# A graph layer with residual and layer norm on one Trainium2 core: broadcasts of packed slots cut into eight, 14 gather buffers, PSUM banks dealt three and two, and late-planned SP transfers

## The chip, the cores and the metric

The kernel runs on one core of a Trainium2 chip. The time is device microseconds for one launch. Before the change the median of three runs is 502.47 us (501.62 to 507.94). One further run was profiled; all views of a profile below come from it.

## The reference, cut to what matters

```python
N, E, D = 6250, 100000, 128          # nodes, edges, features; edges are sorted by dst
def layer(X, src, dst, edge_types, W_data, b_data, W_control, b_control, W_self, b_self):
    Xs = X[src]
    m_data = Xs @ W_data.T + b_data
    m_ctrl = Xs @ W_control.T + b_control
    msg = jnp.where((edge_types == 0)[:, None], m_data, m_ctrl)
    agg = jax.ops.segment_sum(msg, dst, num_segments=X.shape[0])
    return jax.nn.relu(agg + (X @ W_self.T + b_self))
x = _layernorm(x + layer(x, ...), axis=-1)
```

## The kernel before, in words

**Table.** Every node's two messages (data and control) are computed once: 49 blocks of 128 nodes, two blocks at a time (25 steps `q`), as x times the two weights on TensorE (L483), with the result split into three bf16 parts that add up to the f32 value. The parts stay in SBUF as `m3` (98 tiles of 128 rows by 384 columns) and are also stored to DRAM as `table` (L499). A step's product lies in PSUM in a bank of ring `g` or ring `a`.

**Windows.** The first 27 x 160 nodes (`NW`, `WN`) are summed without touching DRAM for each edge. A window of 160 nodes has up to 21 x 128 edges. They are ordered into a grid of 98 source tiles by 32 slots (`R`) in `ranks`: one-hot tiles (`hots`, L681) are summed on TensorE (L692, bank `rk`), VectorE reduces the sums to slot numbers (L706), and matmuls (L742, bank `vt`) drop each edge's source and target into its slot. ScalarE copies the result out (`vs`), SP stores it to DRAM (`packed`, L762), and SP reads one window's 32 x 98 slots back, broadcast to all 128 partitions (`rows`, L893: 784 KB written, one contiguous run of 6272 bytes read 128 times). The windows go in eight groups, `GROUPS = [1, 2] + [4] * 6`: `ranks` and the store are made for a group, the broadcast for a window.

In `sums`, VectorE turns `rows` into a one-hot of source rows (L901) and `to_d` into a one-hot of targets (`hot2`, L909). Then 25 times per window: *stage 1*, up to four matmuls (L922) that pick 128 messages from `m3` into a PSUM bank of ring `g`; a copy to bf16 by ScalarE (L425, `gs`); *stage 2*, seven matmuls (L936, L939) that add them up by target into the window's bank of ring `a`. Edges that find no slot go in a short list: `sr` is gathered from `table` by GpSimd (L851), and SP copies its halves into `gl` (L858), which is the last of the 25 steps.

**Gathered blocks.** The remaining nodes are 16 blocks of 125. For these GpSimd gathers 128 messages at a time from `table` (`t_msg`, L1016, 263 times, 8 buffers) and TensorE adds them by target (L1023, one bank `ga`).

**Closing.** `close` reduces a window's or block's bank over its three parts (L551), adds x (`xr`, loaded at L524 and L531), norms, and stores (L602, L606). The x columns of the own-node product come in `xc`, `xb` and `t_xc` (L887, L534, L1000).

**Order.** Nothing runs in the order of the source. Every operation is handed to `Plan.add` with an engine, a planned duration, a due time and the buffers that it reads and writes. `Plan.run` is a list scheduler: an engine takes, of the operations whose buffers are ready at the earliest possible time, the one with the smallest due; it never waits for a due time. What comes out is one fixed order of instructions for each engine, and on the chip each engine runs its own order, waiting at each instruction for what it needs. So an instruction whose data are later on the chip than in the plan holds up everything behind it on its engine; for SP, which issues nearly all plain transfers, this is everything behind it in the queue. `T0 = 36`, `TW = 13` are the planned start of window 0 and the planned time of a window; `when` is the due time of a group's `ranks`.

PSUM's eight banks are `vt` 1, `rk` 1, `ga` 1, `a` 1 and `g` 4.

Of the kernel before, what the change touches and what calls it, by code (L numbers as in the profile page):

```python
# [21 lines left out]
P = 128  # L22
# [21 lines left out]
R = 32  # L44
# [38 lines left out]
class Op:  # L83
    __slots__ = ("alts", "due", "lat", "deps", "after", "left", "ready", "start", "end", "out",
                 "index", "engine")

    def __init__(self, alts, due, lat):
        self.alts, self.due, self.lat = alts, due, lat
        self.deps, self.after, self.out = [], [], []


class Plan:
    HOP = {"PE": 0.22, "ACT": 0.15, "DVE": 0.11, "POOL": 0.12, "SP": 0.12}
    OWN = {"DVE": 0.09, "ACT": 0.12}
    OTHER = 0.5

    def __init__(self):
        self.ops, self.rings = [], {}

    def add(self, engine, dur, fn, due, r=(), w=(), lat=0.0):  # L100
# [24 lines left out]
        return op  # L125
# [4 lines left out]
    def run(self):  # L130
# [31 lines left out]
        while len(order) < n:  # L162
# [79 lines left out]
def sums_over_windows(ctx, tc, x, xt, edges, w, bias, out, total):  # L242
# [16 lines left out]
    def C(shape, dtype, name):  # L259
        return Buf(plan, const, shape, dtype, name, 1)  # L260

    T0 = 36.0
    TW = 13.0
    LAT = 0.2
    G0, G1 = 0.0, -4
    GC = 1.3
    SPD = 0.45


# [7 lines left out]
    add("ACT", 0.1, lambda: A.dma_start(b1.t, bias), 0.0, [], [b1], lat=2.5)  # L277

# [83 lines left out]
    def count_rows():  # L362
# [8 lines left out]
    vec(0.5, 1, lambda: V.tensor_copy(row_i.t, row_f.t), [row_f], [row_i])  # L371
    er = C([NBD, RL, 3], I32, "er")
    add("POOL", 1.0, lambda: G.indirect_dma_start(
        out=er.t.rearrange("p k c -> p (k c)"), out_offset=None,
        in_=edges.rearrange("(p k) c -> p (k c)", k=RL),
        in_offset=bass.IndirectOffsetOnAxis(ap=row_i.t[:, 0:1], axis=0)),
        0.5, [row_i], [er], lat=3.5)
# [3 lines left out]
    vec(0.6, RL, lambda: V.tensor_copy(dst_f.t, er.t[:, :, 1]), [er], [dst_f])  # L381
    vec(0.6, RL, lambda: V.tensor_scalar(less.t, dst_f.t, bound_p.t, None, op0=ALU.is_lt,
# [15 lines left out]
    def load_edges(b, n, out_, due, buf, key, engine):  # L398
# [13 lines left out]

    left = C([1, D3], F32, "left")
# [3 lines left out]
    add("ACT", 0.4, lambda: A.copy(brows.t[:1], b1.t), 0.5, [b1], [brows])  # L417
    vec(0.5, D3, lambda: V.tensor_sub(left.t, b1.t, brows.t[:1]), [b1, brows], [left])
    add("ACT", 0.4, lambda: A.copy(mid.t, left.t), 0.5, [left], [mid])
    vec(0.5, D3, lambda: V.tensor_sub(brows.t[2 * R : 2 * R + 1], left.t, mid.t), [left, mid],  # L420
        [(brows, 2)])
# [19 lines left out]
    XB = [12, 12, 12, 13]  # L441
    XC = 4 * WN
    xts = []
# [167 lines left out]
    def ranks(gi, w0, nw, when, step, engines):  # L611
# [237 lines left out]
        for pr in range(nh):  # L849
            sr = B(work, [P, D3], BF16, "sr", 2)  # L850
            add("POOL", GC, lambda pr=pr, sr=sr: G.indirect_dma_start(  # L851
                out=sr.t[: room(pr)], out_offset=None, in_=table[:, :],
                in_offset=bass.IndirectOffsetOnAxis(ap=at.t[: room(pr), pr : pr + 1], axis=0)),
                d3 + 1, [(at, pr), table_b], [sr], lat=2.0)
            for i in range(2 * pr, min(2 * pr + 2, nw)):
                q = 64 * (i % 2)
                gl = B(work, [P, D3], BF16, "gl", 8)
                add("SP", SPD, lambda gl=gl, sr=sr, q=q: S.dma_start(gl.t[64:], sr.t[q : q + 64]),  # L858
                    d3 + 2 + pr, [sr], [(gl, "s")], lat=2.0)
                gls.append(gl)  # L860
# [23 lines left out]
    def sums(gi, w0, nw, placed):  # L884
# [5 lines left out]
        for i in range(nw):  # L890
            due = T0 + (w0 + i) * TW
            sp = B(work, [P, R, NT], BF16, "rows", 3, R * NT)
            add("SP", SPD, lambda i=i, sp=sp: S.dma_start(  # L893
                sp.t.rearrange("p r c -> p (r c)"),
                packed[gi, i // 2, (i % 2) * 64 : (i % 2) * 64 + R, :]
                .rearrange("r c -> (r c)")[None, :].to_broadcast([P, R * NT])),
                due - 12, [(packed_b, gi)], [sp], lat=3.0)
            half = R // 2
# [7 lines left out]
            for ci, (c0, c1) in enumerate(zip(cuts, cuts[1:])):  # L906
# [51 lines left out]
    def gathered(bis, when, step):  # L958
# [37 lines left out]
        for j, bi in enumerate(bis):  # L996
# [6 lines left out]
            for k in range(nt):  # L1003
                at = start + step * k
                kk = j * nt + k
                if k % KB == 0:
# [209 lines left out]
```

## Time and profile before

| what | value |
|---|---|
| median of 3 runs | 502.47 us |
| profiled execution: its own time | 505.74 us |
| its span, first to last instruction | 504.2 us |
| mean granted TensorE clock | 0.959 of full |
| TensorE matmul busy | 453.6 us (90%) |
| VectorE, ScalarE busy | 394.9 us (78%), 349.0 us (69%) |
| GpSimd busy | 299.2 us (59%) |
| bytes moved by DMA | 76.83 MB, mean 152 GB/s |
| broadcasts `rows<-packed` | 27 issues, SP, 784 KB each |
| gathers `t_msg<-table` | 263 issues, GpSimd, mean 1057 ns |

TensorE's row counts a matmul from its issue to its modelled end, so a busy TensorE may still have gaps between matmuls; the number of matmuls in a stretch says more. The chain of waits is followed back from the last instruction: at each step to what released it.

### The profile page before, as it was taken

Reading aid. Unit: us, or ns where it says so; the run is one execution under the profiler, and the core shown is the slowest. Engines: PE = TensorE matmul, PEld = TensorE weight load, DVE = VectorE, ACT = ScalarE, POOL = GpSimd, SP = SyncE. Lnnn points to the kernel's source line nnn. Section 1 sums busy time; section 2 is a strip of 40 time slices with the busy share of each in tenths; the row PEclk is TensorE's granted clock in tenths of the full one; section 3 lists DMA queues with packets and bytes.
Section 4 is the critical chain, followed back from the end, with each engine's and each line's share of the span. In section 5 each row is a group of like instructions: output and inputs, shape, how many; then the busy total and the mean of one; then the engine's idle time right before and its main releaser. Section 6 shows DMA issues by size and latency. Waiting matters only on the chain.

```text
span 504.2 us, 26935 instructions
## 1 busy us (share of the span) xinstructions
PE 453.6 (90%) x11461; PEld 364.8 (72%) x11461; DVE 394.9 (78%) x1271; ACT 349.0 (69%) x891; POOL 299.2 (59%) x290
## 2 busy tenths in 40 slices
PE   4999986996999998999699999999899999897990
PEld 2666654884778787787598877878678887686880
DVE  6599987998898988989598899888948787553343
ACT  2476763763767876778486788777867778595881
POOL 1000057775467687857676677777676757776720
PEclk9999996998799999999899999999989999898997
DMA  4399977346552466634655256662654426644320
GB/s 145 122 287 342 292 149 241 100 106 208 143 149 66 132 172 179 179 87 134 195 160 171 64 139 195 200 169 69 195 154 130 153 68 155 225 116 135 79 69 19
DMA packets 63117, 76.83 MB, mean 152 GB/s; under 512 B 21000, under 2 KB 52893, under 8 KB 62989
## 3 DMA queue, kind: packets, MB, share of 16 engines
q1 hardware_dynamic: 49147, 47.35, 29.8%
q0 software_dynamic: 13456, 27.42, 21.3%
q8 instruction: 91, 1.49, 1.2%
q10 hardware_dynamic: 386, 0.26, 0.2%
q14 instruction: 37, 0.30, 0.2%
HBM read 60.50 MB, written 13.17 MB: 146 GB/s over the span
## 4 chain that ended last, share of the span: by engine, by line
PE 67%; DMA 16%; DVE 7%; ACT 5%; issue 2%; SPq 1%; POOL 0%; ACTq 0%; DVEq 0%; POOLq 0%
PE g L922 20%; PE a L936 17%; PE rk L692 8%; DMA rows<-packed 7%; PE ga L1023 7%; DMA t_msg<-table,t_idx 6%; PE g L483 3%; PE a L939 3%; PE vt L742 3%; ACT gs L425 3%; DMA packed<-vs 2%; DVE rows L901 1%; ACT to_d L432 1%; PE ga L692 1%; PE a L508 1%
## 5 line engine op out<-in xcount | busy, mean ns | idle before, releaser
L1016 POOL DMA_INDIRECT t_msg<-table,t_idx x263 | 278.0, 1057 | 113.8 <-PE ga L1023 42.5
L425 ACT CAST gs<-g 128x384 bf16<-128x384 f32 x639 | 270.2, 487 | 103.3 <-PE g L922 81.3
L922 PE MATMUL g<-m,rows 128*32 128x384 bf16 x2646 | 261.2, 338 | 7.2 <-DVE rows L901 5.3
L936 PE MATMUL a<-gs,hot 128*32 128x384 bf16 x2592 | 259.9, 335 | 2.8 <-ACT gs L425 1.9
L922 PEld LDWEIGHTS <-rows 128*32 128x32 bf16 x2646 | 159.5, 135 | 22.2 <-DVE rows L901 6.4
L939 PE MATMUL a<-gs,hot 128*32 128x128 bf16 x1944 | 164.1, 222 | 0.0
L1023 PE MATMUL ga<-t_msg,t_hot 128*32 128x384 bf16 x1036 | 125.7, 332 | 16.7 <-DMA t_msg<-table,t_idx 10.7
L936 PEld LDWEIGHTS <-hot 128*32 128x32 bf16 x2700 | 121.9, 97 | 24.8 <-issue 7.9
L706 DVE TENSOR_REDUCE slot<-rk 128x4 f32<-128x392 f32 (+1 forms) x138 | 76.8, 556 | 23.9 <-PE rk L692 12.5
L939 PEld LDWEIGHTS <-hot 128*32 128x32 bf16 x2025 | 86.8, 99 | 10.7 <-issue 0.7
L692 PE MATMUL rk<-hots,tri 128*32 128x392 bf16 (+1 forms) x588 | 73.1, 327 | 0.7 <-issue 0.7
L692 PE MATMUL rk<-hots,rest 128*32 128x392 bf16 (+1 forms) x556 | 68.6, 328 | 2.6 <-DVE slot L706 2.6
L1023 PEld LDWEIGHTS <-t_hot 128*32 128x32 bf16 x1036 | 53.2, 98 | 23.7 <-issue 19.5
L909 DVE TENSOR_TENSOR hot<-iota_b,to_d 128x1280 bf16<-128x1280 bf16 (+1 forms) x81 | 67.6, 842 | 0.1
L851 POOL DMA_INDIRECT sr<-table,at x14 | 16.7, 1191 | 46.8 <-DMA xr<-in_x 38.6
L901 DVE TENSOR_SCALAR rows<-rows,pid 128x1568 bf16<-128x1568 bf16 x54 | 34.3, 638 | 12.8 <-DMA rows<-packed 12.7
L1010 DVE TENSOR_TENSOR t_hot<-iota_b,t_code 128x768 bf16<-128x768 bf16 (+2 forms) x47 | 24.7, 526 | 19.3 <-PE g L922 11.2
L681 DVE TENSOR_TENSOR hots<-iota_b,st 128x784 bf16<-128x784 bf16 (+1 forms) x83 | 38.6, 487 | 0.5 <-PE vt L742 0.4
L692 PEld LDWEIGHTS <-rest 128*32 128x32 bf16 x624 | 28.1, 98 | 10.6 <-issue 8.3
L692 PEld LDWEIGHTS <-tri 128*32 128x32 bf16 x672 | 30.1, 99 | 3.7 <-issue 1.4
L551 DVE TENSOR_REDUCE s<-a 128x128 f32<-128x384 f32 x27 | 15.0, 557 | 21.2 <-ACT bs L425 7.7
L425 ACT CAST m<-g 128x512 bf16<-128x512 f32 x20 | 11.6, 587 | 13.8 <-PE g L491 13.8
(188 smaller groups left out, 545.4 us busy)
## 6 DMA issues: line engine op xcount, KB each, us to landing
rows<-packed SPq DMA_DIRECT2D x27, 784.0 KB
table<-m SPq DMA_DIRECT2D x12, 768.0 KB
t_msg<-table,t_idx POOLq DMA_INDIRECT x263
rows<-in_xt SPq DMA_DIRECT2D x8, 256.0 KB
xc<-in_xt SPq DMA_DIRECT2D x6, 320.0 KB
gl<-sr SPq DMA_DIRECT2D x27, 48.0 KB
xr<-in_x SPq DMA_DIRECT2D x5, 256.0 KB
out<-xr SPq DMA_DIRECT2D x5, 256.0 KB
```

The source lines that it names most:

```text
L425: [("ACT", act(cols), lambda: A.copy(o(), src())), ("DVE", dve(cols), lambda: V.tensor_copy(o(), src()))], None, None, due, r, w, lat)
L681: lambda k=k, kn=kn, ci=ci, hs4=hs4: V.tensor_tensor(hv(ci)[:, k - ks[ci] : k - ks[ci] + kn].rearrange("p k w (c d) -> p (k w) c d", d=2), ...
L692: T.matmul(acc.t[R * j : R * j + R, c * wide : c * wide + wide], wt.t[:, R * j : R * j + R], one(k).rearrange("p w c -> p (w c)"), start=s ...
L706: vec(due, len(m) * wide, lambda r=r, m=m: V.tensor_reduce(slot.t[:, r:KT:L, :], acc.t[:, : len(m) * wide].rearrange("p (k w c) -> p k w c ...
L901: add("DVE", dve(half * NT, 0.335), lambda sp=sp, rs=rs: V.tensor_scalar(sp.t[:, rs], sp.t[:, rs], pid1.t, None, op0=ALU.is_equal), due - ...
L909: lambda i=i, hot2=hot2, s4=s4, c0=c0, c1=c1: V.tensor_tensor(hot2.t[:, c0:c1].rearrange("p g (c d) -> p g c d", d=2), iota1_b.t.rearrange ...
L922: T.matmul(gp.t[R * t : R * t + R, :D3], sp.t[:, :, 4 * g + t], m3.t[:, 4 * g + t, :], start=True, stop=True)
L936: T.matmul(a.t[R * j : R * j + R, :D3], hot2.t[:, g, R * j : R * j + R], gs.t, start=g == 0, stop=False, skip_group_check=True)
L939: T.matmul(a.t[R * c : R * c + R, D3:], hot2.t[:, g, P:], gs.t[:, c * D : (c + 1) * D], start=False, stop=last, skip_group_check=True)
L1010: vec(at + 1, kn * P, lambda hot=hot, kk=kk, kn=kn, s4=s4: V.tensor_tensor(hot.t.rearrange("p k (c d) -> p k c d", d=2), iota1_b.t[:, :P]. ...
L1016: add("POOL", GC, lambda m=m, kk=kk: G.indirect_dma_start(out=m.t, out_offset=None, in_=table[:, :], in_offset=bass.IndirectOffsetOnAxis(a ...
L1023: T.matmul(ga.t[R * i : R * i + R, :D3], hot.t[:, k % KB, R * i : R * i + R], m.t, start=k == 0, stop=False, skip_group_check=True)
```

## The change

Six things are edited together.

1. The broadcast of a window's slots is issued as eight transfers (`RP`) of 16 partitions each, due 0.9 us apart from 14 us ahead of the window, in place of one due 12 us ahead. VectorE's L901 still needs all of them.
2. `t_msg` has 14 buffers in place of 8. To make room in SBUF, the biases `b1` and `left` now lie in the ring of `two`, and the edge rows `er` in the ring of `xc`.
3. Ring `a` has two PSUM banks in place of one, ring `g` three in place of four; the table's steps are dealt 10 to `a` and 15 to `g` (5 and 20 before).
4. The planner adds a `slack` to the time at which an SP operation with a due time over 60 counts as ready: 6 us for loads of edges and x and for stores, 3 us for `gl`, 2 us for the store of `packed`; and 3 us for the gather of `sr` on GpSimd. It moves the operation back in SP's or GpSimd's order; no instruction is added for it.
5. The planned extra latency of a ScalarE or VectorE copy out of PSUM (`LAT`) is 0.1 in place of 0.2.
6. `when` is 0 in place of 3 for group 0 and 8 in place of 18 for group 1.

```diff
+    SLACK = dict.fromkeys(("t_raw", "win", "xc", "t_xc", "xr", "xrg", "xb", "out"), 6.0)
+    SLACK.update(gl=3.0, packed_b=2.0)
+    FROM = 60.0
...
+        kind = [(i[0] if isinstance(i, tuple) else i).name for i in w] or ["out"]
+        if engine == "SP" and due > self.FROM:
+            op.slack = self.SLACK.get(kind[0], 0.0)
...
-                    o.ready = max(o.ready, op.end + lag)
+                    o.ready = max(o.ready, op.end + lag + o.slack)
...
-    LAT = 0.2
+    LAT = 0.1
+    RP, RA, RS = 8, 14, 0.9
...
-    b1 = C([1, D3], F32, "b1")
+    early = lambda: B(work, [P, 48 * R], BF16, "two", 2, 48 * R)
+    b1_, left_ = early(), early()
...
-    er = C([NBD, RL, 3], I32, "er")
+    er_ = B(work, [P, XC], F32, "xc", 2, XC)
...
-        mp = B(ps, [P, 512], F32, *(("a", 1) if q % 5 > 3 else ("g", 4)))
+        mp = B(ps, [P, 512], F32, *(("a", 2) if q % 5 > 2 else ("g", 3)))
...
-                d3 + 1, [(at, pr), table_b], [sr], lat=2.0)
+                d3 + 1, [(at, pr), table_b], [sr], lat=2.0).slack = 3.0
...
-            add("SP", SPD, lambda i=i, sp=sp: S.dma_start(
-                sp.t.rearrange("p r c -> p (r c)"),
-                packed[gi, i // 2, (i % 2) * 64 : (i % 2) * 64 + R, :]
-                .rearrange("r c -> (r c)")[None, :].to_broadcast([P, R * NT])),
-                due - 12, [(packed_b, gi)], [sp], lat=3.0)
+            for j in range(RP):
+                add("SP", SPD, lambda i=i, sp=sp, j=j: S.dma_start(
+                    sp.t[P // RP * j : P // RP * (j + 1)].rearrange("p r c -> p (r c)"),
+                    packed[gi, i // 2, (i % 2) * 64 : (i % 2) * 64 + R, :]
+                    .rearrange("r c -> (r c)")[None, :].to_broadcast([P // RP, R * NT])),
+                    due - RA + RS * j, [(packed_b, gi)], [(sp, ("p", j))], lat=2.0)
...
-            a = B(ps, [P, 512], F32, "a", 1)
+            a = B(ps, [P, 512], F32, "a", 2)
...
-                gp = B(ps, [P, 512], F32, "g", 4)
+                gp = B(ps, [P, 512], F32, "g", 3)
...
-                m = B(work, [P, D3], BF16, "t_msg", 8)
+                m = B(work, [P, D3], BF16, "t_msg", 14)
...
-            when, step, engines = 3.0, 0.9, ["SP"]
+            when, step, engines = 0.0, 0.9, ["SP"]
         elif gi == 1:
-            when, step, engines = 18.0, 1.1, ["SP", "ACT"]
+            when, step, engines = 8.0, 1.1, ["SP", "ACT"]
```

More of the change, by code (lines that the diff above doesn't have):

```diff
@@ L84 @@
     __slots__ = ("alts", "due", "lat", "deps", "after", "left", "ready", "start", "end", "out",
-                 "index", "engine")
+                 "index", "engine", "slack")
     def __init__(self, alts, due, lat):
-        self.alts, self.due, self.lat = alts, due, lat
+        self.alts, self.due, self.lat, self.slack = alts, due, lat, 0.0
         self.deps, self.after, self.out = [], [], []
@@ L260, in C @@
         return Buf(plan, const, shape, dtype, name, 1)
+    XC = 4 * WN
     T0 = 36.0
     TW = 13.0
-    LAT = 0.2
+    LAT = 0.1
     G0, G1 = 0.0, -4
@@ L274, in sums_over_windows @@
     w_sb = C([D, D3], F32, "w_sb")
-    b1 = C([1, D3], F32, "b1")
+    early = lambda: B(work, [P, 48 * R], BF16, "two", 2, 48 * R)
+    b1_, left_ = early(), early()
+    b1 = lambda: b1_.t.bitcast(F32)[:1, :D3]
+    left = lambda: left_.t.bitcast(F32)[:1, :D3]
     add("ACT", 0.1, lambda: A.dma_start(w_sb.t, w), 0.0, [], [w_sb], lat=2.5)
-    add("ACT", 0.1, lambda: A.dma_start(b1.t, bias), 0.0, [], [b1], lat=2.5)
+    add("ACT", 0.1, lambda: A.dma_start(b1(), bias), 0.0, [], [b1_], lat=2.5)
     iota_f = C([P, P], F32, "iota_f")
@@ L371, in sums_over_windows @@
     vec(0.5, 1, lambda: V.tensor_copy(row_i.t, row_f.t), [row_f], [row_i])
-    er = C([NBD, RL, 3], I32, "er")
+    er_ = B(work, [P, XC], F32, "xc", 2, XC)
+    er = lambda: er_.t.bitcast(I32)[:NBD, : RL * 3].rearrange("p (k c) -> p k c", c=3)
     add("POOL", 1.0, lambda: G.indirect_dma_start(
-        out=er.t.rearrange("p k c -> p (k c)"), out_offset=None,
+        out=er_.t.bitcast(I32)[:NBD, : RL * 3], out_offset=None,
         in_=edges.rearrange("(p k) c -> p (k c)", k=RL),
         in_offset=bass.IndirectOffsetOnAxis(ap=row_i.t[:, 0:1], axis=0)),
-        0.5, [row_i], [er], lat=3.5)
+        0.5, [row_i], [er_], lat=3.5)
     dst_f = C([NBD, RL], F32, "dst_f")
@@ L380, in sums_over_windows @@
     in_row = C([NBD, 1], F32, "in_row")
-    vec(0.6, RL, lambda: V.tensor_copy(dst_f.t, er.t[:, :, 1]), [er], [dst_f])
+    vec(0.6, RL, lambda: V.tensor_copy(dst_f.t, er()[:, :, 1]), [er_], [dst_f])
     vec(0.6, RL, lambda: V.tensor_scalar(less.t, dst_f.t, bound_p.t, None, op0=ALU.is_lt,
@@ L410, in load_edges @@
         add(engine, dur, fn, due, [first] if b else [], [(buf, key)], lat=2.0)
-    left = C([1, D3], F32, "left")
     mid = C([1, D3], BF16, "mid")
@@ L416, in sums_over_windows @@
     vec(0.2, D3, lambda: V.memset(brows.t, 0.0), [], [brows], 0.3)
[L417 to L420, printed above, removed]
+    add("ACT", 0.4, lambda: A.copy(brows.t[:1], b1()), 0.5, [b1_], [brows])
+    vec(0.5, D3, lambda: V.tensor_sub(left(), b1(), brows.t[:1]), [b1_, brows], [left_])
+    add("ACT", 0.4, lambda: A.copy(mid.t, left()), 0.5, [left_], [mid])
+    vec(0.5, D3, lambda: V.tensor_sub(brows.t[2 * R : 2 * R + 1], left(), mid.t), [left_, mid],
         [(brows, 2)])
@@ L441, in sums_over_windows @@
     XB = [12, 12, 12, 13]
-    XC = 4 * WN
     xts = []
```

## The prediction

> **What bounds the kernel now.** I read the head of the page first, then busy time in equal stretches of 20 us, the waits of TensorE, the chain of waits in order of time, and the waits of SP's queue.
>
> ```profile
> span 504.2 us, 26935 instructions
> PE 453.6 (90%) x11461; PEld 364.8 (72%) x11461; DVE 394.9 (78%) x1271; ACT 349.0 (69%) x891; POOL 299.2 (59%) x290
> PEclk9999996998799999999899999999989999898997
> ```
>
> TensorE is busy for 90% of the span and no other engine comes near, so time can only come out of TensorE's gaps and of the slices where its granted clock falls below 9 tenths. The stretches say where these lie; the first column after the times is TensorE busy, with its matmuls in brackets, and the clock stands behind POOL.
>
> ```profile
> 60.00:80.00 20.00, 14.98 (x373) 10.57 (x366) 15.84 (x68) 10.61 (x32) 10.16 (x11) 0.91 0.79 214
> 80.00:100.00 20.00, 18.75 (x445) 14.35 (x448) 17.46 (x45) 12.79 (x30) 14.73 (x15) 0.83 0.54 139
> 120.00:140.00 20.00, 16.54 (x364) 11.92 (x368) 15.63 (x46) 10.51 (x27) 11.56 (x10) 0.74 0.60 194
> 240.00:260.00 20.00, 16.26 (x419) 14.01 (x422) 13.90 (x40) 11.71 (x30) 14.04 (x15) 0.91 0.65 188
> 260.00:280.00 20.00, 20.00 (x573) 17.22 (x565) 18.57 (x45) 14.67 (x38) 12.63 (x12) 1.00 0.49 140
> ```
>
> 260 to 280 is TensorE undisturbed: 573 matmuls. I take 573 per 20 us as its pace and price a disturbed stretch by the matmuls missing, which counts the gap and the slow clock after it together. 60 to 80 lost 20 x (1 - 373/573) = 7.0 us, 80 to 100 lost 4.5, 120 to 140 lost 7.3, 240 to 260 lost 5.4. By the same view 360 to 380 (459 matmuls) lost 4.0, 420 to 440 (426) 5.1 and 440 to 460 (487) 3.0. That is 36 us in seven stretches. The kind of matmul differs between stretches, so each is good to perhaps 1.5 us. The chain names what ended last in each:
>
> ```profile
> 69.59 4.30 DMA packed<-vs
> 73.91 5.89 DMA rows<-packed
> ...
> 116.47 2.15 DMA packed<-vs
> 118.64 6.13 DMA rows<-packed
> ...
> 234.80 8.90 DMA t_msg<-table,t_idx
> ...
> 358.38 7.75 DMA t_msg<-table,t_idx
> ...
> 421.41 2.46 DMA packed<-vs
> 423.88 5.25 DMA rows<-packed
> ...
> 451.51 1.17 SPq L531
> 453.19 4.96 DMA rows<-packed
> ```
>
> So there are three kinds of stall: a group's slots packed too late (70, 117, 421), a gather that lands too late (235, 358), and a broadcast issued late because SP stood at x loads in front of it (451).
>
> ```profile
> SPq L1000 <- PE ga L511: 59.2, 7, 23.1
> SPq L602 <- DVE xr L594: 40.3, 3, 27.4
> SPq L858 <- DMA sr<-table,at: 33.1, 9, 8.0
> ```
>
> These rows are SP standing still with a queue behind it, up to 27.4 us at once.
>
> **Group 1 earlier.** Its first store is issued at 69.59 and window 1 starts at 81.25, while the table's last step ends on VectorE at about 59. With `when` 10 us smaller, its instructions come earlier in VectorE's and TensorE's order, and the store should go out by about 58. What they push back is the table: VectorE is busy 19.15 of 20 us between 40 and 60, so the part of group 1 that now runs after 62 (six of L727 and L733 at about 0.5 us, a dozen small ones at about 0.17) delays it by some 5 us, of which TensorE, whose own share of group 1 is done in that time, gives back about 1.5. Of the 11.5 us lost from 60 to 100 I take 8 as saved (bounds 0, if the table is delayed by all of it, and 11.5). Group 2's chain needs the `rk` bank and `hots` that group 1 then frees sooner; I take half of the 7.3 us, 3.5 (bounds -3 and 7.3). Group 0's step from 3 to 0 puts at most eight short VectorE instructions (0.16 to 0.18 us each) before L420, for which TensorE waits at the start; 0 to +1, taken as 0.
>
> **Gathers.** One GpSimd gather takes 0.95 us and 0.30 to the next, so 8 buffers are 10 us of lead and 14 are 17.5. A gather that needs 8.9 us beside two broadcasts is then covered. Both stretches come back nearly whole: 8 of 9.4 us, and 2 more for a smaller stall behind the 7.01 us gather at 188 (bounds 5 and 11.4). GpSimd itself is not next: 277 gathers at 1.25 us from 66 end at 412, some 70 us before they do now.
>
> **SP's order.** With slack, x loads and stores stand behind the broadcasts. That is 2.5 of the 3.0 us at 440 to 460. For the late store at 421 the planner's 2 us help only by order: 1.5 of 5.1. Bounds together 0 and 8.1. The slack issues nothing; what is late next is a store or an x load, whose buffers turn over once in two groups, and GpSimd's `sr` gather, needed a window later.
>
> **Eight transfers.** 189 more issues at the median 0.383 us of L893 are 72 us of SP, hidden by its standing still (133 us in the three rows above). If that cover is gone, two broadcasts at a group's start hold what stands behind them for 16 x 0.383 - 0.8 = 5.3 us: `gl`, `xc`, x. VectorE's L901 must wait for up to eight semaphores; the one semaphore instruction that it has there took 50 ns, so 27 x 7 x 0.05 = 9.5 us of an engine with 109 us to spare. The time to land is not in the trace. From below: seven issues at the shortest 0.326 and a small transfer at 2.15 (the 49 KB store), 4.4 us. From above: seven at 0.47 (L531) and 4.30, 7.6 us. One transfer takes 4.96 to 8.78 on the chain, mostly about 5.9. So -1.5 to +1.7 at some six places, -9 to +10; I take 0, since the path by median issue (2.7 + 2.15) is a little shorter and the queue longer.
>
> The Trainium skill speaks against this edit: "DMA: Bandwidth & Descriptors", section "Rules for kernel authors", says to coalesce small transfers into one large one and not to split one by partition halves, since both use the same 16 engines; the same page's fit of 2.0 us plus bytes over 436 GB/s gives an estimate of 3.8 us for one and, if eight followed each other, 17.9 us. This case's row has three broadcasts issued within 1.28 us at 118.64 without waiting for each other, so they overlap; by the serial reading the sum below would be some 70 us worse.
>
> **Banks.** Table steps still find five banks. A second `a` bank lets a window start before the last one is reduced (L551, 0.557 us, and the copy of 0.265); but TensorE's waits for this are 0.2 us in all, so 0 to -5, taken as 0. The third `g` bank less: stage 1 at 0.338 us and the copy at 0.487 make 0.83 us per bank, or 0.28 us per step with three, under the planner's 0.385 us of TensorE per step. So the banks do not set the pace, but ScalarE's other work between two copies (`to_d`, `slot`, `xr`, `xrg`, `bs`, `vs`, `s`, `to`: 50 us together in the groups by engine) has 0.33 us of cover instead of 0.71. Bounds 0 and +50 if all of it reached TensorE; the nearest row, TensorE waiting for ScalarE's `gs`, is 0.8 + 1.9 us now. I take +4. `LAT` only tightens the planned order and goes with this.
>
> **Buffers shared.** `b1` and `left` are done at 7.3 and `two` is first written at 28.6; `er` is read last at 18.3. Group 1's `xc` must then wait for that, but SP stands until 19.36 at the first table store anyway. 0; up to +3 if an x load of the table stands behind it.
>
> **The sum.** 8 + 3.5 + 8 + 2 + 2.5 + 1.5 = 25.5 saved, 4 paid: 504.2 - 21.5 = 482.7 us of span. The run lay 1.5 us above its span and the median of the runs 3.3 below that run, so 482.7 + 1.5 - 3.3 = 481 us.
>
> **The rivals.**
>
> *The stall moves.* Group 1 comes first, the table and so the gathers end later, and groups 1 and 2 are as late as ever against the windows. For it: VectorE's 19.15 of 20. Against it: VectorE has 4 of 20 us free from 60 to 80. Then the 11.5 us of the first two terms are gone: 492.5 us.
>
> *Three banks starve TensorE* (the slower side). Every interruption of ScalarE reaches it: with 40 of the 50 us exposed, 504.2 - 25.5 + 40 = 518.7 of span, 517 us. It passes the time before from 25.5 us exposed on, and 2% from about 36. Against it: ScalarE waits 81.3 us for stage 1 as it is.
>
> *It does not do what it says.* The plan's times are too short anyway (13 us planned for a window, some 15 taken), so that a few us of slack leave the order on the chip nearly as late as it was, and only the gathers gain, against the banks' price and one new stall: 504.2 - 10 + 4 + 4 = 502.2, or 500.5 us.
>
> **How the numbers follow.** Forecast 0.6, with a range of its own from 471 to 492; stall moves 0.18; does not do it 0.12; starving 0.1. A measurement of this kernel tells about 2% from no change, so faster means under 492.4 and slower over 512.5. Faster: 0.58 + 0.08 = 0.66. Same: 0.02 + 0.1 + 0.11 = 0.23. Slower: 0.1 + 0.01 = 0.11. The range of 8 in 10 takes in the second and the last rival: 465 to 508.
>
> **What would show it.** Right: the row of L1023 waiting for `t_msg` falls from 10.7 to under 2 us; no `packed<-vs` followed by `rows<-packed` near 70 on the chain; the stretch 120 to 140 over 480 matmuls; SP's long rows (L1000, L602) shorter; the mean clock above 0.96. Wrong: TensorE waiting for `gs` for over 10 us, or the end of the table (the first L1016) later than 72 us with window 1 still after 80.

## The result, and the profile after

The changed kernel takes 533.76 us (median of 4 runs, 533.43 to 534.08) against 503.63 us of the kernel before (4 runs): the ratio is 1.0586 [1.0513, 1.0659]. It is 30 us slower, where 481 was predicted. Lines have moved by 10 or 11: the broadcast's issue is now L904 (L893 before), VectorE's one-hot of the rows L912 (L901), the slot sums on TensorE L702 (L692), their reduction on VectorE L716 (L706), the gather L1027 and the matmuls that wait for it L1034.

Of the changed kernel, called after, the head of its profile's page and the row of the queue that carries the broadcasts:

```profile
span 531.8 us, 27272 instructions
PE 460.0 (86%) x11461; PEld 367.1 (69%) x11461; DVE 394.9 (74%) x1274; ACT 354.2 (67%) x888; POOL 301.8 (57%) x290
PEclk9999989999899999899989999898999989989996
...
q1 hardware_dynamic: 52171, 47.36, 39.6%
```

TensorE, VectorE and ScalarE have about the work they had; the span has grown around them. TensorE's idle time is 531.8 - 460.0 = 71.8 us, against 504.2 - 453.6 = 50.6 before. The mean granted clock is 0.967 against 0.959, so a lower clock is not the cause. The last row is the queue of SP's transfers (packets, MB, share of the 16 engines' span): the same 47.36 MB as before, but before they took 29.8% of 504.2 us and now 39.6% of 531.8, which is 150 us and 211 us for each of 16 engines. 52171 packets stand against 49147: the difference, 3024, is 189 more transfers with 16 packets each.

The stretches, in the columns of the prediction (TensorE busy with its matmuls in brackets, weight loads, VectorE, ScalarE, GpSimd, clock, DMA share, GB/s):

```profile
60.00:80.00 20.00, 14.80 (x360) 10.78 (x357) 15.69 (x52) 11.45 (x33) 8.63 (x8) 0.91 0.89 169
...
120.00:140.00 20.00, 13.68 (x352) 10.12 (x343) 12.64 (x39) 9.70 (x25) 15.73 (x15) 1.00 1.04 189
240.00:260.00 20.00, 17.90 (x494) 14.60 (x487) 14.58 (x50) 16.51 (x43) 15.73 (x15) 1.00 0.91 175
260.00:280.00 20.00, 17.21 (x435) 14.00 (x437) 14.27 (x38) 11.31 (x28) 15.34 (x16) 0.91 0.71 161
```

The DMA share is highest where TensorE has least to do: 0.89 and 1.04 in 60 to 80 and 120 to 140 (the share adds up the times of packets, so above 1 some of them overlap on an engine). Yet they move little: 169 GB/s at a share of 0.89, where before it was 214 GB/s at 0.79 (60 to 80). And 260 to 280, undisturbed before with 573 matmuls, has 435. That a byte now takes more DMA time is the first sign.

The waits of all engines (us in all, times, longest):

```profile
DVE rows L912 <- DMA rows<-packed: 40.9, 17, 4.3
PE rk L702 <- DVE slot L716: 27.8, 15, 4.3
...
PE a L947 <- ACT gs L436: 4.8, 12, 0.8
```

From the chain of waits of after, in order of time, from 66 to 143 us (start, duration, what):

```profile
66.71 4.12 DMA rows<-packed
70.84 6.50 DMA rows<-packed
77.36 4.95 DMA xr<-in_x
82.31 0.62 DVE rows L912
...
122.66 7.21 DMA rows<-packed
...
133.98 4.73 DMA rows<-packed
138.89 0.63 DVE rows L912
139.51 0.48 DVE hots L691
...
141.51 0.49 DVE slot L716
142.04 0.52 PE rk L702 x4
```

Before, VectorE waited 12.7 us for `rows<-packed` and TensorE 2.6 us for `slot`. Now it is 40.9 and 27.8. Where group 1 starts, the pieces of two windows and an x load queued behind them land last, up to 82.31. The last five pieces of the chain show how one wait becomes the other: a broadcast lands, VectorE does the rows, then what its order has behind them, then the reduction that TensorE needs for the next group's slots. VectorE's own order at that place (start, duration, idle time before it in brackets):

```profile
132.97 1.55 DVE L920 TENSOR_TENSOR hot<-iota_b,to_d 128x1280 bf16<-128x1280 bf16 x2
134.44 0.56 DVE L716 TENSOR_REDUCE slot<-rk 128x4 f32<-128x392 f32 x1
138.89 0.63 DVE L912 TENSOR_SCALAR rows<-rows,pid 128x1568 bf16<-128x1568 bf16 x1 [3.89 <-DMA rows<-packed]
139.43 0.56 DVE L691 TENSOR_TENSOR hots<-iota_b,st 128x784 bf16<-128x784 bf16 x1
139.92 0.81 DVE L912 TENSOR_SCALAR rows<-rows,pid 128x1568 bf16<-128x1568 bf16 x1
...
141.44 0.55 DVE L716 TENSOR_REDUCE slot<-rk 128x4 f32<-128x392 f32 x1
```

Two reductions are 7.0 us apart, 3.9 of them VectorE's wait for a broadcast whose window is not the one that TensorE is held up for.

The wait that the gathers' buffers were to remove is gone here. Its row of the groups by line (busy, mean ns | idle time before, what ended most of it):

```profile
L1034 PE MATMUL ga<-t_msg,t_hot 128*32 128x384 bf16 x1036 | 101.4, 332 | 0.8 <-DMA t_msg<-table,t_idx 0.4
```

TensorE waits 0.4 us for gathered rows, 10.7 before. That is not the buffers' work alone: the kernels below that have the same 14 buffers and are faster have 2.5 to 7.9 us of this wait.

### The profile page after: what moved, and what is told of

It is laid out like the page before. It is cut to its first block, busy times and chain, and to the rows that moved or that the text cites. A ratio compares the mean times of both kernels' runs of the same rounds, so it can differ in the third digit from the quotient of the medians.

```text
span 531.8 us, 27272 instructions
## 1 busy us (share of the span) xinstructions
PE 460.0 (86%) x11461; PEld 367.1 (69%) x11461; DVE 394.9 (74%) x1274; ACT 354.2 (67%) x888; POOL 301.8 (57%) x290
## 3 DMA queue, kind: packets, MB, share of 16 engines
q1 hardware_dynamic: 52171, 47.36, 39.6%
## 4 chain that ended last, share of the span: by engine, by line
PE 53%; DMA 22%; SPq 8%; DVE 7%; issue 4%; ACT 4%; ACTq 0%; DVEq 0%; POOL 0%
PE g L933 16%; DMA rows<-packed 15%; PE a L947 14%; PE rk L702 6%; SPq L904 6%; PE ga L1034 5%; PE a L950 3%; PE vt L752 2%; DVE rows L912 2%; ACT gs L436 2%; DMA sr<-table,at 1%; DMA packed<-vs 1%; PE g L493 1%; DMA xc<-in_xt 1%; DMA xr<-in_x 1%
## 5 line engine op out<-in xcount | busy, mean ns | idle before, releaser
L1027 POOL DMA_INDIRECT t_msg<-table,t_idx x263 | 281.3, 1070 | 171.2 <-PE ga L1034 55.7
L436 ACT CAST gs<-g 128x384 bf16<-128x384 f32 x640 | 275.0, 481 | 108.3 <-PE g L933 91.8
L947 PE MATMUL a<-gs,hot 128*32 128x384 bf16 x2592 | 255.6, 335 | 10.8 <-ACT gs L436 4.8
L933 PEld LDWEIGHTS <-rows 128*32 128x32 bf16 x2646 | 163.6, 135 | 20.4 <-issue 6.1
L947 PEld LDWEIGHTS <-hot 128*32 128x32 bf16 x2700 | 118.1, 97 | 42.4 <-issue 24.9
L1034 PE MATMUL ga<-t_msg,t_hot 128*32 128x384 bf16 x1036 | 101.4, 332 | 0.8 <-DMA t_msg<-table,t_idx 0.4
L950 PEld LDWEIGHTS <-hot 128*32 128x32 bf16 x2025 | 82.7, 98 | 11.1 <-issue 5.9
L716 DVE TENSOR_REDUCE slot<-rk 128x4 f32<-128x392 f32 (+1 forms) x138 | 76.2, 553 | 17.5 <-PE rk L702 13.0
L912 DVE TENSOR_SCALAR rows<-rows,pid 128x1568 bf16<-128x1568 bf16 x54 | 34.8, 655 | 61.4 <-DMA rows<-packed 40.9
L702 PE MATMUL rk<-hots,rest 128*32 128x392 bf16 (+1 forms) x556 | 55.5, 330 | 28.6 <-DVE slot L716 27.8
L702 PE MATMUL rk<-hots,tri 128*32 128x392 bf16 (+1 forms) x588 | 61.3, 326 | 0.0
L702 PEld LDWEIGHTS <-rest 128*32 128x32 bf16 x624 | 25.6, 96 | 40.5 <-issue 37.4
L1034 PEld LDWEIGHTS <-t_hot 128*32 128x32 bf16 x1036 | 48.1, 98 | 6.2 <-issue 1.9
L702 PEld LDWEIGHTS <-tri 128*32 128x32 bf16 x672 | 28.3, 99 | 2.6
L752 PEld LDWEIGHTS <-two 128*64 128x64 bf16 x567 | 14.7, 111 | 7.3 <-DVE two L743 2.7
```

The lines of the kernel that those rows point to most:

```text
L436: [("ACT", act(cols), lambda: A.copy(o(), src())), ("DVE", dve(cols), lambda: V.tensor_copy(o(), src()))], None, None, due, r, w, lat)
L702: T.matmul(acc.t[R * j : R * j + R, c * wide : c * wide + wide], wt.t[:, R * j : R * j + R], one(k).rearrange("p w c -> p (w c)"), start=s ...
L716: vec(due, len(m) * wide, lambda r=r, m=m: V.tensor_reduce(slot.t[:, r:KT:L, :], acc.t[:, : len(m) * wide].rearrange("p (k w c) -> p k w c ...
L912: add("DVE", dve(half * NT, 0.335), lambda sp=sp, rs=rs: V.tensor_scalar(sp.t[:, rs], sp.t[:, rs], pid1.t, None, op0=ALU.is_equal), due - ...
L933: T.matmul(gp.t[R * t : R * t + R, :D3], sp.t[:, :, 4 * g + t], m3.t[:, 4 * g + t, :], start=True, stop=True)
L947: T.matmul(a.t[R * j : R * j + R, :D3], hot2.t[:, g, R * j : R * j + R], gs.t, start=g == 0, stop=False, skip_group_check=True)
```

## The experiments

Each theory's expectation stands as it was written ahead of the run. The kernels were run on several chips; each ratio is against the kernel before on the same chip, run beside it. Where times of different chips are compared, the kernel before itself differs: 499.1 to 503.63 us, and 651 us on two chips.

**Is it the cut, and nothing else of the change?** Four kernels on one chip, where the kernel before took 499.1 us. *undo_split* is the changed kernel with the one transfer of before:

```diff
...
-            for j in range(RP):
-                add("SP", SPD, lambda i=i, sp=sp, j=j: S.dma_start(... [P // RP, R * NT])),
-                    due - RA + RS * j, [(packed_b, gi)], [(sp, ("p", j))], lat=2.0)
+            add("SP", SPD, lambda i=i, sp=sp: S.dma_start(... [P, R * NT])),
+                due - 12, [(packed_b, gi)], [sp], lat=3.0)
```

> The changed kernel with each window's slots broadcast in one transfer again (due 12 us ahead, planned latency 3.0); buffers, banks, slack, earlier groups and LAT stay changed. Theory 'the cut': eight pieces land some 4 us later than one (7 to 11 us from first issue to last packet in the trace after, against 4 to 5 before) and VectorE stands at them (40.9 us); undone, the time falls by 25 to 45 us, to 490 to 508 us, and VectorE's wait for rows<-packed falls under 15 us. Rival 'the order': slack, earlier groups and banks have put the planned order out of step, and the broadcasts are only where it shows; then this stays within 525 to 538 us.

Measured: 483.29 us, ratio 0.967 [0.9613, 0.9727], below the range of either theory; the direction is that of the cut. *split_alone* is the kernel before with only the cut, in the lines of the change:

> The kernel before with the cut alone, planned as in the change (eight pieces of 16 partitions, due from 14 us ahead by 0.9, planned latency 2.0). Theory 'the cut': 515 to 535 us, with VectorE's wait for rows<-packed over 25 us. Rival 'the order': 498 to 508 us.

Measured: 559.57 us, 1.1183 [1.1119, 1.1247], more than either theory said. So the cut alone costs 60 us, and without it the rest of the change gains 16. But both let the planner make another order, so they do not yet tell the transfers from the order. The other two keep an order and change only what SP issues in it. *one_in_place* has the order of after, with the whole broadcast issued at the first piece's place and nothing at the other seven:

```diff
...
-                add("SP", SPD, lambda i=i, sp=sp, j=j: S.dma_start(
-                    sp.t[P // RP * j : P // RP * (j + 1)].rearrange("p r c -> p (r c)"),
+                add("SP", SPD, lambda i=i, sp=sp, j=j: j or S.dma_start(
+                    sp.t.rearrange("p r c -> p (r c)"),
...
-                    .rearrange("r c -> (r c)")[None, :].to_broadcast([P // RP, R * NT])),
+                    .rearrange("r c -> (r c)")[None, :].to_broadcast([P, R * NT])),
```

> The changed kernel in its own planned order, except that SP issues the whole broadcast where the first of its eight pieces stood, and nothing for the other seven. Theory 'the cut': 488 to 508 us. Rival 'the order': 520 us or more, since the order is that of the changed kernel.

Measured: 483.5 us, 0.9699 [0.9624, 0.9775], again a little below the range of the cut's theory. *split_in_place* has the order of before; where SP issued one broadcast, it issues eight pieces in a row:

```diff
...
+            def spread(i=i, sp=sp):
+                for j in range(8):
+                    S.dma_start(sp.t[16 * j : 16 * j + 16] ... .to_broadcast([16, R * NT]))
+            add("SP", SPD, spread, due - 12, [(packed_b, gi)], [sp], lat=3.0)
```

> The kernel before in its own planned order, instruction by instruction on every engine, except that where SP issues one broadcast it issues eight pieces in a row. Whatever it costs is the chip's price of the cut and no question of planning. Theory 'the cut': 510 to 530 us, mean time of a 6272-byte packet from 276 ns to 400 ns or more. Rival 'the order': within 498 to 508 us.

Measured: 582.41 us, 1.1695 [1.1591, 1.1798], well above what was expected. Its waits:

```profile
DVE rows L903 <- DMA rows<-packed: 54.1, 14, 8.3
PE rk L692 <- DVE slot L706: 28.6, 9, 6.3
```

With the order held, the transfers' own form is worth 50 us in the one order and 83 in the other. (The two runs behind the 50 did not stand beside each other; by their ratios, 1.0586 and 0.9699, it is 44.) Eight issues in SP's queue in place of one, each with a semaphore of its own, and a piece's 98 KB where a window's 784 KB went in one are all that differs. In the order of after, VectorE's wait is gone with one transfer. The waits of one_in_place:

```profile
PE ga L1034 <- DMA t_msg<-table,t_idx: 7.6, 9, 3.7
...
PE rk L702 <- DVE slot L716: 2.2, 7, 0.6
```

VectorE's wait for the rows is no longer among the waits that the profile lists; TensorE's for `slot` fell from 27.8 to 2.2. TensorE's busy time is 443.9 in a span of 481.5: against 460.0 in 531.8 that is 34 us less idle and 16 us less busy, together the 50.

**What makes eight transfers slower than one?** The trace has a record for each packet; the 6272-byte ones are a window's run for one partition, 3456 in every kernel. The trace does not say which DMA engine a packet ran on; dealt out evenly, 128 partitions in one transfer give each of the 16 engines eight of them in a row, 16 partitions only one. The mean time of one, and the median over 27 windows from the first issue to the end of the last packet, worked out from these records (the shortest is 236 ns in all):

| kernel | transfers per window | a packet, ns | first issue to last packet, us | time, us |
|---|---|---|---|---|
| before | 1 | 276 | 5.2 | 503.63 |
| one_in_place | 1 | 293 | 5.0 | 483.5 |
| four_in_place | 4 | 393 | 7.3 | 502.0 |
| one_big_seven_small | 8, one of 112 partitions | 334 | 7.0 | 514.95 |
| distinct_one | 1 | 293 | 5.5 | 480.53 |
| distinct_eight | 8 | 452 | 9.0 | 525.38 |
| after | 8 | 503 | 10.0 | 533.76 |
| split_in_place | 8 | 541 | 8.5 | 582.41 |

The same records in order of their start within a window say more. In one_in_place the first 16 packets of a window take 369 ns and the other 112 take 282; in after the first 16 take 392 and the last 16 take 569. So even one transfer begins with slow packets, and where a window is cut, the pieces that come later are slower than the first.

Four more kernels, on a chip where the kernel before took 501.12 us, ask why. The first two have the order of after; the last two wait for early parts of the table besides and share an order of their own. The theory: a packet that an engine does alone costs more than one of several in a row. Its rivals: the count of transfers itself, and many engines reading the same addresses at once. *four_in_place* issues 32 partitions at every second piece's place:

```diff
...
+                    lo, hi = 16 * j, 16 * j + (0 if j % 2 else 32)
```

> The changed kernel's own order, with four transfers of 32 partitions at the places of pieces 0, 2, 4 and 6. One transfer took 483.5 us (293 ns for a 6272-byte packet), eight take 533.8 (503 ns). Theory 'a lone packet on each DMA engine is slow': two packets for each engine and transfer overlap in part, so 485 to 505 us and a mean packet of 330 to 430 ns. Rival 'the number of issues': half of the 189 extra ones is left (81), so half of the 50 us, 500 to 515, and the packet near 300 ns.

Measured: 502.0 us, 1.0024 [0.9972, 1.0077], and 393 ns for a packet. The time lies in both ranges (485 to 505 and 500 to 515), so it decides nothing; the packet does, since the 300 ns of the rival did not come. *one_big_seven_small* keeps 216 issues and lets one transfer carry 112 of the 128 partitions:

```diff
...
+                    lo, hi = [0, 112, 114, 116, 118, 120, 122, 124][j], [112, 114, 116, 118, 120, 122, 124, 128][j]
```

> The changed kernel's own order and its 216 issues, but the first of a window's eight transfers carries 112 partitions and the other seven 2 to 4. Theory 'a lone packet on each DMA engine is slow': most of the data go as seven packets in a row on each engine, so 484 to 505 us. Rival 'the number of issues' (SP's time, the semaphores that VectorE and SP wait for): 525 us or more, as with eight equal pieces.

Measured: 514.95 us, 1.0289 [1.0172, 1.0405], between the two and in neither range. The packets are nearly as short as with one transfer (334 ns), and yet 31 us of the 50 are lost. Its page's row of the broadcasts' queue:

```profile
q1 hardware_dynamic: 49579, 47.35, 32.3%
```

Its waits, of VectorE and TensorE:

```profile
DVE rows L915 <- DMA rows<-packed: 31.3, 14, 4.5
PE rk L702 <- DVE slot L716: 17.1, 13, 5.0
```

And the waits of SP's own queue:

```profile
SPq L907 <- DMA rows<-packed: 45.9, 22, 4.3
...
SPq L1014 <- DMA rows<-packed: 18.4, 5, 4.3
```

SP, which issues the transfers, stands 64 us waiting for earlier pieces to land before it issues the next. In the changed kernel the row of L904 is 13.7 us (26 times).

The semaphores in the trace show who asks for it. SP's transfers take eight semaphores in turn, with few exceptions, and most issues first wait on their own semaphore, until the transfer eight issues earlier has landed. So the program as built allows SP eight transfers under way: eight whole broadcasts or loads before, the pieces of a single window now. Worked out from these records, SP stands 79.9 us at such waits in one_big_seven_small, 24.7 in after and 0.2 in one_in_place.

So the number of transfers has a price besides the packets'. Neither theory alone gives this kernel; both act, and the runs do not divide the 50 us between them.

*distinct_eight* and *distinct_one* let each partition read a run of its own, 6272 bytes of `table`, in eight transfers and in one; the window sums are then not the reference's.

```diff
...
+                            table.rearrange("a b -> (a b)").rearrange("(p c) -> p c", c=R * NT)[lo:hi])
```

> The changed kernel's eight transfers a window, but each partition reads a run of 6272 bytes of its own (the first 128 such runs of the table) in place of the one run that all share; the window sums are then not the reference's. Theory 'lone packet': the packet stays at 450 to 550 ns and the time near 530 us. Rival 'the same address': sixteen DMA engines that read the same bytes at the same moment slow each other; with runs of their own the packet falls under 330 ns and the time under 505 us.

> As the one before, in one transfer for a window: the packet's time when each engine has eight runs of its own in a row. Theory 'lone packet': 240 to 320 ns, about 483 us. Rival 'the same address': also under 300 ns, since the sharing is gone here too; it is the base for the run with eight.

Measured, one run each: 525.38 and 480.53 us; packets of 452 and 293 ns. Reading the same addresses is not the cause: different addresses take eight transfers nearly as badly.

**Does VectorE's fixed order turn the late landing into lost time?** *split_told* is the changed kernel with nothing but a number of the planner changed: a piece is planned to take 6.5 us in place of 2.0, so that VectorE's order has the rows later, behind reductions that can already be done.

```diff
...
-                    due - RA + RS * j, [(packed_b, gi)], [(sp, ("p", j))], lat=2.0)
+                    due - RA + RS * j, [(packed_b, gi)], [(sp, ("p", j))], lat=6.5)
```

It ran on three chips. On the first two the kernel before itself takes 651 us (below), on the third 503.17.

> The changed kernel, with one number altered: the planned time from a piece's issue to its landing is 6.5 us in place of 2.0, which is nearer to what the trace shows (first issue to last packet, median of the 27 windows, 10.0 us). Theory 'VectorE stands in its order': the loss is carried by VectorE, which by the plan reaches the one-hot of rows before the pieces have landed, and holds up the slot reductions behind it; told the truth, the plan puts other VectorE work first, and the time is 495 to 515 us with the wait for rows<-packed under 20 us. Rival 'the transfers themselves bound it': 528 us or more.

> As split_told, on another chip: 6.5 us planned from a piece's issue to its landing in place of 2.0. Theory 'VectorE stands in its order': 495 to 515 us, the wait of the one-hot of rows for rows<-packed under 20 us. Rival 'the transfers themselves bound it': 528 us or more.

> As split_told. Where the kernel before takes about 500 us: theory 'VectorE stands in its order' 495 to 515 us, rival 'the transfers themselves bound it' 528 us or more. Where it takes about 650 us, it is compared with the next kernel alone: by the theory within 2% of it, by the rival 5% or more above it.

Measured on the third: 510.75 us, 1.0143 [1.0059, 1.0228], against 1.0586 of the changed kernel. Its page:

```profile
span 508.0 us, 27283 instructions
...
q1 hardware_dynamic: 52171, 47.36, 41.3%
```

Its waits:

```profile
DVE rows L912 <- DMA rows<-packed: 3.0, 6, 1.5
PE rk L702 <- DVE slot L716: 5.0, 6, 2.0
```

The transfers are as many and as slow as in after (501 ns a packet), but VectorE waits 3.0 us for them in place of 40.9, and TensorE 5.0 for `slot` in place of 27.8. That brings back 23 us: with the transfers unchanged, the planned order alone carried nearly half of the loss. The new number moves instructions on other engines too, so the 23 us belong to the new order as a whole; that VectorE's wait is the main thing in it is argued from these two rows. *nosplit_base* is undo_split again, beside it:

> The changed kernel with the broadcast in one transfer, the base of the three runs that undo one more part each, in case the chip is again one of those on which the kernel before takes 650 us. By the prediction's terms it is then 10 us or more under the runs that undo the buffers or the earlier groups, and some 4 us above the run that undoes the banks; where the kernel before takes 500 us, it is 481 to 486 us again.

Measured: 481.56 us, 0.9559 [0.9499, 0.962]. So 29 us separate eight transfers planned rightly from one. By the stretches, half of it lies early: from 60 to 160 us split_told_c has 2000 matmuls and nosplit_base 2429, which is 20 x 429/573 = 15 us, with a granted clock of 0.66 in its 80 to 100; from 160 to 280 they are level (3272 and 3261). One part can be read, among TensorE's waits of split_told_c:

```profile
PE a L947 <- DMA gl<-sr: 4.6, 1, 4.6
```

In nosplit_base this wait is not there. Fourteen pieces stand ahead of that load in SP's queue and hold it for 11.8 us, 4.3 of them at one semaphore; in nosplit_base two whole broadcasts take 1.95. The stretch from 80 to 100 has 255 matmuls against 475, 7.7 us. What the rest of the 29 us is made of stays open.

**The three other terms one by one.** nosplit_undo_when, nosplit_undo_bufs and nosplit_undo_banks are undo_split with `when` at 3 and 18, with 8 buffers of `t_msg`, and with rings of 4 and 1 banks.

```diff
...
-            when, step, engines = 8.0, 1.1, ["SP", "ACT"]
+            when, step, engines = 18.0, 1.1, ["SP", "ACT"]
...
-                m = B(work, [P, D3], BF16, "t_msg", 14)
+                m = B(work, [P, D3], BF16, "t_msg", 8)
...
-            a = B(ps, [P, 512], F32, "a", 2)
+            a = B(ps, [P, 512], F32, "a", 1)
...
```

> The changed kernel with the broadcast in one transfer (483.3 us) and, besides, the due times of the first two groups' ranks back at 3 and 18. By the prediction's sum these were worth 8 + 3.5 us: 490 to 498 us. Rival: the gain came from the gathers and SP's order alone: 481 to 486.

> The changed kernel with the broadcast in one transfer (483.3 us) and 8 buffers of gathered rows in place of 14. By the prediction's sum the buffers were worth 10 us: 489 to 497 us, with TensorE's wait for t_msg up from 7.9. Rival: with the broadcasts earlier in SP's order, 8 buffers are enough: 481 to 486.

> The changed kernel with the broadcast in one transfer (483.3 us) and the PSUM banks at four for g and one for a again. By the prediction's sum the new deal cost 4 us: 477 to 482 us. Rival: the second bank of a gives more than the fourth of g: 486 to 495.

All three were run twice, on the two chips on which the kernel before takes 651 us:

| kernel | first chip, us | ratio | second chip, us | ratio |
|---|---|---|---|---|
| nosplit_undo_when | 691.85 | 1.0598 [1.0541, 1.0656] | 692.05 | 1.0639 [1.0559, 1.0718] |
| nosplit_undo_bufs | 663.35 | 1.019 [1.0152, 1.0227] | 663.35 | 1.0177 [1.0099, 1.0255] |
| nosplit_undo_banks | 671.24 | 1.0295 [1.0256, 1.0334] | 670.18 | 1.0293 [1.0199, 1.0387] |
| split_told | 691.49 | 1.0612 [1.0574, 1.065] | 689.38 | 1.0611 [1.0525, 1.0697] |

The second runs had these expectations:

> As nosplit_undo_when, on another chip. By the prediction's sum 490 to 498 us, with the broadcast in one transfer (483.3 us) as the base; rival: 481 to 486.

> As nosplit_undo_bufs, on another chip. By the prediction's sum 489 to 497 us; rival (8 buffers are enough once the order is better): 481 to 486.

> As nosplit_undo_banks, on another chip. By the prediction's sum 477 to 482 us; rival (the second bank of a is worth more than the fourth of g): 486 to 495.

The times repeat to 2 us, but they are inconclusive for the question. undo_split itself was not run on these two chips, and even kernels with most of the change's gain are slower than the kernel before there, so a ratio does not carry over: split_told has 1.061 there and 1.014 on the other chip. What can be read is a difference within these chips: leaving `when` as before costs 28 us more than leaving the buffers. How much each of the three brings on the chips where the kernel takes 500 us was not measured.

**The best version.** The changed kernel with its broadcast in one transfer, run as undo_split and as nosplit_base, takes 0.967 and 0.9559 of the kernel before and beats both kernels.

## Why the prediction was wrong

The step that failed is the part "Eight transfers" with its "I take 0". The term was worth about 50 us (533.76 against 483.5 in the same order; 44 by the ratios), where its bounds were -9 to +10. Three of its sentences failed in turn.

*The landing.* It was bounded at 7.6 us from issue to landing, as seven issues and one small transfer of 4.30. Measured are 10.0 us from the first issue to the last packet, at the median. The seven issues took 4.6 us and not 2.7 (0.66 us from one to the next, not 0.383: an issue itself takes 0.42, and some wait on their semaphore), and the pieces, with one packet for each engine if they are dealt out evenly, 503 ns a packet and not 276. The small transfer that the bound rested on was a store of 49 KB and had no such packets.

*What hides the issues.* SP's standing still was to cover 72 us of issuing. Where a group starts it does not. There the timeline of SP's queue (start, duration) reads in after:

```profile
65.26 10.53 SPq L904 DMA_DIRECT2D rows<-packed  x16
```

and in one_in_place, in the same order:

```profile
65.62 0.84 SPq L904 DMA_DIRECT2D rows<-packed  x2
```

The text had 5.3 us for what stands behind two broadcasts; it is 9.7. Each of the last eight issues waits for a piece of the window before it, a wait that the text did not count. The load of `gl` behind them goes out at 83.93 in place of 76.97.

*Whom a late landing costs.* The text priced a later broadcast at some six places, as if only its own window waited. VectorE's 109 us to spare were taken as cover, but an engine with a fixed order has none at the instruction where it waits: its wait went on to the slot reductions behind it, and from there to TensorE, for whichever group was being packed. When the planner was told 6.5 us, both waits fell (40.9 to 3.0 and 27.8 to 5.0) and 23 of the 50 us came back. Only the semaphores' own cost was right: the instructions at L912 took 50 ns at the median.

The Trainium skill's rule, cited there from "DMA: Bandwidth & Descriptors", section "Rules for kernel authors", was set aside and had the right sign: it says to use one transfer over 128 partitions and not two over halves. The size did not hold: by that page's fit (section "Anatomy of one DMA — SWDGE (gpsimd) path"), which it gives for transfers issued by GpSimd, eight one after the other would land after an estimated 17.8 us. Measured on SP's queue are 10.0, so they overlap, though the later pieces' packets are slower (392 to 569 ns). The 70 us that the text put on the serial reading were nearer to the 50 than its 0.

Everything else held in the sum. Without the cut the span is 480.7 (undo_split), 479.8 (nosplit_base) and 481.5 (one_in_place), where the sum had 482.7; the medians are 483.29, 481.56 and 483.5 where it had 481. Against the kernel before on the same chip they are 15.8, 21.6 and 15.6 us less, where the text had 21.5. The prediction's own count, the matmuls missing from 573, shows which terms agree, against the trace of before, which was not taken beside these runs. The stretches of one_in_place:

```profile
60.00:80.00 20.00, 17.04 (x433) 12.39 (x432) 19.39 (x58) 12.33 (x34) 9.91 (x10) 1.00 0.71 212
80.00:100.00 20.00, 19.41 (x524) 15.42 (x520) 19.51 (x57) 14.71 (x35) 15.43 (x16) 1.00 0.47 121
120.00:140.00 20.00, 19.51 (x558) 16.86 (x554) 19.15 (x53) 14.75 (x37) 16.32 (x13) 1.00 0.61 169
240.00:260.00 20.00, 19.77 (x546) 16.03 (x540) 16.15 (x42) 15.58 (x41) 15.48 (x15) 1.00 0.60 176
360.00:380.00 20.00, 19.33 (x542) 17.01 (x536) 15.84 (x43) 14.96 (x40) 15.38 (x16) 1.00 0.59 177
420.00:440.00 20.00, 19.65 (x564) 16.58 (x561) 12.88 (x35) 17.93 (x47) 15.71 (x15) 1.00 0.58 175
440.00:460.00 20.00, 20.00 (x562) 18.32 (x556) 8.32 (x25) 18.68 (x49) 13.32 (x14) 1.00 0.30 81
```

- *Group 1 earlier*: 60 to 100 lost 4.9 + 1.7 = 6.6 us in place of 11.5, so 4.9 came back where 8 was taken. Its store went out at 61.59 where the text said about 58; the store's place on the chain near 70 is gone.
- *Group 2*: 120 to 140 lost 0.5 in place of 7.3: 6.8 came back, near the upper bound of 7.3, where 3.5 was taken.
- *Gathers*: 240 to 260 and 360 to 380 lost 0.9 and 1.1 in place of 5.4 and 4.0: 7.4 came back of the 8 taken. But TensorE's waits for `t_msg` as such did not fall below 2 us as the text said: 7.6 in one_in_place, 7.9 in undo_split, 2.5 in nosplit_base. They lie elsewhere now.
- *SP's order*: 420 to 440 lost 0.3 and 440 to 460 lost 0.4, in place of 5.1 and 3.0: 7.4 came back where 4.0 was taken. SP's rows behind `xr` and `ga` fell from 40.3 and 59.2 to 24.0 and 20.4 us.
- In all 26.5 us came back in these stretches by this count, where 23.5 were taken (the 25.5 of the sum hold 2 more for the stall at 188, which lies outside them). That the sum came out is in part luck: group 1 gave 3.1 less than taken, group 2 and SP's order 3.3 and 3.4 more. The span fell by 22.7, so some 4 us were lost elsewhere. That is what *Banks* was to cost, though no run shows that it is the banks. TensorE waits 4.5 us for `gs` (1.9 before), so "three banks starve TensorE" did not happen, in this kernel or in after (4.8).

Work sits earlier in these stretches than before by as much as the kernel is faster, so each of these is good to an us or two only.

Of the rivals, none named the cause. The slower side had ScalarE's copies as its mechanism; it came from a term that the text had set to zero. Of the signs that the prediction named, "the stretch 120 to 140 over 480 matmuls" told it: 352. The clock above 0.96, the shorter wait for `t_msg` and the shorter of SP's rows (L1011, 17.2 us in place of 59.2) came out as said, in a kernel that is slower.

## What to carry to other kernels

A transfer cut into pieces is not free because its bytes are the same: price the pieces by their own packets, ask how many each DMA engine gets in a row, and bound a landing by a transfer of the same shape, not by a small one of another. Spare time of an engine in total covers nothing at the one instruction where it must wait; before an edit that can make data later, list what stands behind the waiting instruction in its engine's fixed order, and who waits for that. Count how many transfers the program lets an engine have under way: eight pieces used up what eight whole transfers had. If a planner made the order, its idea of the landing (2.0 us planned, 10 us from the first issue to the last piece's end on the chip) is part of the edit.

## What was not expected of the hardware

A packet of 6272 bytes took 276 to 300 ns at the mean where a window came in one transfer (on the chips where the kernel takes 500 us), 393 where it came in four and 452 to 541 where it came in eight equal ones. The DMA engines' busy share rises with it, so a high share is no proof of much data: 0.89 at 169 GB/s.

SP waited for earlier transfers to land before it issued more, 64 us in one_big_seven_small with its 216 pieces. These are waits on semaphores that the built program holds; the kernel's source names none of them.

On two of the chips the kernel before took 650.78 and 651.14 us, some 150 more than on the others. The page of nosplit_undo_bufs, from the first of them:

```profile
span 661.0 us, 26930 instructions
PE 524.1 (79%) x11461; PEld 373.1 (56%) x11461; DVE 399.5 (60%) x1273; ACT 360.5 (55%) x889; POOL 285.9 (43%) x290
```

Its waits:

```profile
PEld L946 <- issue: 131.3, 203, 2.3
...
PE a L946 <- ACT gs L436: 44.3, 77, 1.7
PE a L946 <- issue: 34.5, 47, 2.1
```

VectorE and ScalarE take their usual time, but weight loads in stage 2 stand 131 us waiting for nothing that the profile shows (15.1 in undo_split on another chip), and TensorE 44.3 for `gs` (5.1). Why these chips differ was not found.
